# Cross-attention block: the mask of the first two pairs laid into PSUM by TensorE, and the maximum taken and subtracted by VectorE

## The chip, the cores and the metric

The kernel runs on one NeuronCore of a Trainium2 chip. The metric is the device time of one execution in microseconds (us), on that core. The core's engines work side by side, each through its own instruction stream in program order: TensorE (PE in the profile; its weight loads are PEld), VectorE (DVE), ScalarE (ACT), GpSimd (POOL) and SyncE (SP, which here only issues transfers). TensorE's results go to PSUM, which the kernel uses in banks of 512 fp32 values per partition (four singly, four as two pairs); VectorE and ScalarE read them from there.

## The reference, cut to what matters

One cross-attention block over 128 sequences of 128 tokens with 256 features and 16 heads of 16 features each, then a feed-forward network. Everything is fp32.

```python
q = (query @ Wq + bq)  # k, v from the context, in the same way; 16 heads
scores = jnp.einsum('bhqd,bhkd->bhqk', q, k) / jnp.sqrt(jnp.float32(D_K))
allowed = j < i + mask                    # mask is 0: strictly below the diagonal
scores = jnp.where(allowed, scores, NEG_INF)
attn = jax.nn.softmax(scores, axis=-1)
attn = attn.at[:, :, 0, :].set(0.0)
ctx = jnp.einsum('bhqk,bhkd->bhqd', attn, v)
x = layer_norm(query + ctx @ Wo + bo, ln1_g, ln1_b)
out = layer_norm(x + relu(x @ W1 + b1) @ W2 + b2, ln2_g, ln2_b)
```

## The kernel before

The 128 sequences are worked on in 64 **pairs** p of two sequences. The kernel's Python code writes out, engine by engine, one fixed order of instructions: each call in the main part appends to the streams of the engines that it uses, and an instruction that waits holds up what stands behind it in its stream. So the order of the calls is the schedule. Pairs 0 and 1 and the beginning of pair 2 have an order of their own, written out call by call (lines 681 to 784); after that `step(p)` repeats for p = 2 to 62, each step working on three pairs at different stages, and a last part (from line 911) drains.

The attention of one pair is split into two halves of the queries. The **high half** (`hi` = 1) holds queries 64 to 127 of both sequences on the 128 partitions, against all n = 128 keys; the **low half** (`hi` = 0) holds queries 0 to 63 against n = 64 keys, since the later keys are masked for them. For each half:

- `scores` (line 316) takes two tiles `pss` of two PSUM banks each (`sps[0]`, `sps[1]`) and fills them with 32 small matmuls; each of the four strips r of 32 rows writes into its own bank. The tiles come from a pool of two (`ps_2`), so a half can't begin before both tiles of the half before it have been read by all their readers. The other four banks (`ps_1`) serve everything else, in turns.
- `mask` (line 340), once per tile t, is a VectorE instruction that adds the mask tile `neg` (0 or -1e30) to the scores and writes `sm` in SBUF. After it the tile of PSUM is free.
- `maximum` (line 352) reduces `sm` to the negated maximum `nmx` on VectorE (line 356), and Pool adds it to `sm` (line 357). `ONE` and `TWO` are the two groups of eight heads of the high half, `ALL` all sixteen heads of the low half.
- `exponential` (line 362) runs on ScalarE, `sums` (line 368) on VectorE (a sum and a reciprocal) and Pool (the product, line 378).
- For pairs 0 and 1 `turn_on_pe` (line 410) turns the probabilities with TensorE transposes `ptp` and ScalarE copies `pT`; later pairs go through VectorE and transfers. `weigh` (line 428) multiplies them with the values into `pc`, `context` copies them, `attention_out` (`po`) applies Wo, and `attention_sum`, `attention_stats` and `norm1` make the first layer norm, whose result `x1` is turned (`turn_x1_on_pe`, `ptn`) for `hidden` (`ph`) and `second` (`py`), the feed-forward network.

Projections are `queries` (`pq`, then `qT` on ScalarE), `keys` (`pk`, `kT`) and `values` (`pv`, then `values_out` on ScalarE: two copies `vz`, a transfer issued on ScalarE's queue, a copy `vd`).

At the very start, TensorE runs 12 transposes of the identity into a bank `warm` that nobody reads (line 682), then the transposes `ptx` and `ptc` of pair 0's tokens, its projections and `scores(0, 1)`. The tile `neg` is made by Pool (lines 166 to 172).

Of the kernel before, what the change touches and what calls it, by code (L numbers as in the profile page):

```python
# [10 lines left out]
ALU = mybir.AluOpType  # L11
AX = mybir.AxisListType

P = 128
# [5 lines left out]
def tile_cross_attention_block(  # L20
# [22 lines left out]
    nc = tc.nc  # L43
# [5 lines left out]
    KC = D // P  # L49
    FC = DFF // P  # L50
    TP = 2 * P
    NS = P // 32
    HH = H // 2
    NP = B // 2
    HP = P // 2
# [19 lines left out]
    states = {}  # L75
# [62 lines left out]
    ident = const.tile([P, P], F32, tag="ident", name="ident")  # L138
# [27 lines left out]
    neg = const.tile([P, 2, HP], F32, tag="neg", name="neg")  # L166
# [46 lines left out]
    def bank(name):  # L213
        return ps_1.tile([P, 512], F32, tag="ps1", name=name)

    def pair(name):
        return ps_2.tile([P, 2, 512], F32, tag="ps2", name=name)
# [24 lines left out]
    def tokens(p, which):  # L242
        st = states.setdefault(p, {})
        st[which + "T"] = proj.tile([P, KC, TP], F32, tag=which + "T", name=f"{which}T_{p}")
        nc.vector.transpose(
            st[which + "T"], blocks_of.pop((which, p)).rearrange("p k u f -> p k (u f)")
        )
# [18 lines left out]
    def queries(p):  # L266
        st = states[p]
        st["qT"] = proj.tile([P, KC, TP], F32, tag="qT", name=f"qT_{p}")
        pq = project(wq, st["xT"], f"pq_{p}")
        for m in range(KC):  # L270
            nc.scalar.activation(  # L271
                st["qT"][:, m, :], pq[:, m * TP : (m + 1) * TP], AF.Identity,
                bias=bqs_c[:, m : m + 1], scale=QSCALE,
            )

    def keys(p):
        st = states[p]
        st["kT"] = proj.tile([P, KC, 2, TP], F32, tag="kT", name=f"kT_{p}")
        pk = project(wk, st["cT"], f"pk_{p}")
        for m in range(KC):  # L280
            for e in range(2):
                nc.scalar.activation(  # L282
                    st["kT"][:, m, e, :], pk[:, m * TP : (m + 1) * TP], AF.Identity,
                    bias=bkh[:, m, e : e + 1], scale=half[:, e : e + 1],
                )
# [27 lines left out]

    def scores(p, hi):

        st = states[p]
        n = P if hi else HP
        sps = [pair(f"pss{hi}_{p}_{t}") for t in range(2)]  # L320
        for m in range(KC):
            for s in range(2):
                first = s * P
                for r in range(NS):
                    strip = slice(32 * r, 32 * r + 32)
                    nc.tensor.matmul(  # L326
                        sps[r // 2][
                            s * HP : (s + 1) * HP, r % 2, m * 2 * n : (m + 1) * 2 * n
                        ].rearrange("p (e j) -> p e j", e=2),
                        st["qT"][strip, m, first + hi * HP : first + hi * HP + HP],  # L330
                        st["kT"][strip, m, :, first : first + n],
                        start=True, stop=True,
                    )
        st["sps", hi] = sps
        st["sm", hi] = soft.tile(
            [P, H, n], F32, tag=f"sm{hi}", name=f"sm{hi}_{p}", bufs=2
        )
        st["nmx", hi] = small.tile([P, H], F32, tag=f"nmx{hi}", name=f"nmx{hi}_{p}")

    def mask(p, hi, t):  # L340
        st = states[p]
        part = slice(t * HH, (t + 1) * HH)
        n = P if hi else HP
        no = neg.rearrange("p u j -> p (u j)") if hi else neg[:, 1, :]
        nc.vector.tensor_tensor(  # L345
            st["sm", hi][:, part, :].rearrange("p (r n) j -> p r n j", r=2),
            st["sps", hi][t][:, :, : 4 * n].rearrange("p r (n j) -> p r n j", j=n),
            no[:, None, None, :].to_broadcast([P, 2, 4, n]),
            ALU.add,
        )  # L350

    def maximum(p, hi, part):
        st = states[p]
        n = P if hi else HP
        sm, nmx = st["sm", hi], st["nmx", hi]
        nc.vector.tensor_reduce(nmx[:, part], sm[:, part, :], AX.X, ALU.max, negate=True)  # L356
        nc.gpsimd.tensor_tensor(  # L357
            sm[:, part, :], sm[:, part, :],
            nmx[:, part, None].to_broadcast([P, part.stop - part.start, n]), ALU.add,
        )  # L360

    def exponential(p, hi, part):
        sm = states[p]["sm", hi]
        nc.scalar.activation(sm[:, part, :], sm[:, part, :], AF.Exp)  # L364

    ALL, ONE, TWO = slice(0, H), slice(0, HH), slice(HH, H)

    def sums(p, hi, part):

        st = states[p]  # L370
        sm = st["sm", hi]
        n = sm.shape[2]
        su = small.tile([P, H], F32, tag=f"su{hi}", name=f"su{hi}_{p}_{part.start}")
        rs = small.tile([P, H], F32, tag=f"rs{hi}", name=f"rs{hi}_{p}_{part.start}")
        su, rs = su[:, part], rs[:, part]
        nc.vector.tensor_reduce(su, sm[:, part, :], AX.X, ALU.add)  # L376
        nc.vector.reciprocal(rs, su)  # L377
        nc.gpsimd.tensor_tensor(  # L378
            sm[:, part, :], sm[:, part, :],
            rs[:, :, None].to_broadcast([P, part.stop - part.start, n]), ALU.mult,  # L380
        )
# [28 lines left out]
    def turn_on_pe(p, hi, ts):  # L410

        st = states[p]
        sm = st["sm", hi].rearrange("p h j -> p (h j)")
        if "pT" not in st:
            pT = soft.tile([P, NS, (H + HH) * 32], F32, tag="pT", name=f"pT_{p}")
            st["pT"] = pT.rearrange("p i (n a) -> p i n a", a=32)
        for t in ts:
            pt = bank(f"ptp{hi}_{p}_{t}")
            for i in range(4):
                at = (4 * t + i) * P  # L420
                nc.tensor.transpose(pt[:, i * P : (i + 1) * P], sm[:, at : at + P], ident)
            n = 4 * t if hi else H + 4 * t
            nc.scalar.copy(  # L423
                st["pT"][:, :, n : n + 4, :].rearrange("p i n a -> p n i a"),
                pt.rearrange("p (n i a) -> p n i a", i=NS, a=32),
            )
# [63 lines left out]
    def attention_sum(p):  # L490
        st = states[p]
        t1 = st["t1"] = ffn.tile([P, 2, D], F32, tag="t1", name=f"t1_{p}")
        nc.vector.tensor_tensor(
            t1, st.pop("po").rearrange("p (s d) -> p s d", s=2), st.pop("xb"), ALU.add
        )

    def attention_stats(p):
        stats(p, states[p]["t1"], 1)
        deviation(p, 1)
# [105 lines left out]
    def add_values(ps):  # L605
        nc.vector.scalar_tensor_tensor(bov_r, ps[:, :D], live, bo_r, ALU.mult, ALU.add)
# [72 lines left out]


    warm = bank("warm")
    for i in range(12):
        nc.tensor.transpose(warm[:, i % 4 * P : (i % 4 + 1) * P], ident, ident)
    states[0] = {}
    for which, first in (("x", tokens_of[0][:, 0:2]), ("c", c_first[:, 0:2])):
        st = states[0]
        st[which + "T"] = proj.tile([P, KC, TP], F32, tag=which + "T", name=f"{which}T_0")
        pt = transposed(first, f"pt{which}_0")
        nc.vector.tensor_copy(st[which + "T"].rearrange("p k i -> p (k i)"), pt)
# [14 lines left out]
    for m in range(KC):  # L704
        pk = bank(f"pk_0_{m}")
        for k in range(KC):
            nc.tensor.matmul(
                pk[:, :TP], wk[:, k, m * P : (m + 1) * P], st["cT"][:, k, :],
                start=(k == 0), stop=(k == KC - 1),
# [16 lines left out]
    for which, first in (("x", tokens_of[0][:, 2:4]), ("c", c_first[:, 2:4])):  # L726
        st = states[1]
# [2 lines left out]
        nc.scalar.copy(st[which + "T"].rearrange("p k i -> p (k i)"), pt)  # L730
    values(0)
    values_out(0)
    mask(0, 1, 0)
    maximum(0, 1, ONE)
    mask(0, 1, 1)
    maximum(0, 1, TWO)
    exponential(0, 1, ONE)
    queries(1)
    scores(0, 0)
    mask(0, 0, 0)  # L740
    mask(0, 0, 1)
    maximum(0, 0, ALL)
    exponential(0, 1, TWO)
    sums(0, 1, ONE)
    keys(1)
    sums(0, 1, TWO)
    exponential(0, 0, ALL)
    values(1)
    ps_bv = fold_values()
    sums(0, 0, ALL)  # L750
    scores(1, 1)
    mask(1, 1, 0)
    add_values(ps_bv)
    maximum(1, 1, ONE)
    turn_on_pe(0, 1, range(2))
    values_out(1)
    turn_on_pe(0, 1, range(2, 4))
    mask(1, 1, 1)
    maximum(1, 1, TWO)
    add_bo(0)  # L760
    turn_on_pe(0, 0, range(2))
    tokens(2, "x")
    scores(1, 0)
    exponential(1, 1, ONE)
    weigh(0)
    context(0)
    mask(1, 0, 0)
    mask(1, 0, 1)
    maximum(1, 0, ALL)
    tokens(2, "c")  # L770
    attention_out(0)
    exponential(1, 1, TWO)
    sums(1, 1, ONE)
    attention_sum(0)
    attention_stats(0)
    exponential(1, 0, ALL)
    queries(2)
    sums(1, 1, TWO)
    keys(2)
    norm1(0)  # L780
# [130 lines left out]
    p = NP - 1  # L911
# [34 lines left out]
    p = NP - 1  # L946
# [34 lines left out]
    st = states[NP - 1]  # L981
    t2 = ffn.tile([P, 2, D], F32, tag="t2", name="t2_last")
    for s in range(2):
        py = bank(f"py_last_{s}")
        for f in range(FC):
            nc.tensor.matmul(
                py[:, :D], st["hT"][:, f, s * P : (s + 1) * P], w2[:, f, :],
                start=(f == 0), stop=(f == FC - 1),
# [46 lines left out]
```

## Time and profile before

| what | us |
|---|---|
| median of 3 runs | 1587.69 |
| lowest and highest run | 1587.53, 1588.26 |
| the profiled execution | 1589.6 |
| its span, from first to last instruction | 1587.9 |
| granted TensorE clock, mean | 1.00 |

The profile describes the one profiled execution. Its span is 1.7 us shorter than that execution's own time, and its time is 1.9 us above the median of the runs that were taken without a profile, so differences of a few us between kernels are read from places within the span, not from the totals. A line of the timeline has a start, a duration, the engine, the source line, the operation, the tile written and the tile read with their shapes, a count (xN: N instructions merged) and, in brackets, how long the engine had been idle before and who released it. Matmuls overlap in the pipeline: a row's duration is longer than the distance from its start to the next start, and the starts are what to measure by.

### The profile page before, as it was taken

What the parts mean: (1) busy time and instruction counts of PE and PEld (TensorE: products, weight loads), DVE (VectorE), ACT (ScalarE), POOL (GpSimd) and SP (SyncE); (2) the same over time, 40 slices, a digit from 0 to 9 for tenths busy, and PEclk for the clock granted to TensorE, in tenths of its full rate; (3) what the DMA queues carried; (4) which work ended last, traced back from release to release, by engine and by line L of the source; (5) the groups of instructions that cost most, each with busy time, mean ns of one, the idle gap of its engine ahead of it and who ended that gap; (6) DMA issues with size and microseconds to landing.
All of it is one profiled execution on the core that took longest, in us unless ns stands there. A gap on an engine that the chain in (4) does not pass through costs nothing.

```text
span 1587.9 us, 41272 instructions
## 1 busy us (share of the span) xinstructions
PE 1574.0 (99%) x16512; PEld 1327.2 (84%) x16512; DVE 1372.9 (86%) x1990; ACT 757.1 (48%) x1498; POOL 1281.9 (81%) x1104
## 2 busy tenths in 40 slices
PE   8999999999999999999999999999999999999998
PEld 6788888888888888888888888888888888888887
DVE  7999888888888988898898988888889989889872
ACT  5555445444444454454444544544444455445442
POOL 7878888788887888888888888888888888888883
PEclk9999999999999999999999999999999999999999
DMA  9555665655556556556556565565555655654521
GB/s 198 108 137 126 151 143 120 147 124 136 147 126 144 137 125 157 138 121 148 129 135 150 127 146 127 118 157 130 138 133 124 154 147 121 144 137 108 127 78 34
DMA packets 479935, 210.12 MB, mean 132 GB/s; under 512 B 348672, under 2 KB 448256, under 8 KB 479744
## 3 DMA queue, kind: packets, MB, share of 16 engines
q1 hardware_dynamic: 371104, 134.29, 38.3%
q10 hardware_dynamic: 108640, 73.19, 17.9%
q8 instruction: 131, 2.15, 0.6%
q14 instruction: 60, 0.49, 0.1%
HBM read 70.00 MB, written 33.03 MB: 65 GB/s over the span
## 4 chain that ended last, share of the span: by engine, by line
PE 92%; DVE 2%; DMA 2%; POOL 1%; SPq 1%; issue 1%; ACT 0%; ACTq 0%; POOLq 0%; DVEq 0%
PE ph L646 27%; PE py L664 26%; PE pq L260 7%; PE po L467 7%; PE pv L292 7%; PE pk L260 6%; PE pss L326 6%; PE pc L448 3%; PE pc L438 2%; DMA pT<-tb 1%; SPq L406 1%; DMA x1t<-tbx 0%; DVE sm L345 0%; DVE su L376 0%; DMA vd<-vz 0%
## 5 line engine op out<-in xcount | busy, mean ns | idle before, releaser
L357 POOL TENSOR_TENSOR sm<-sm,nmx 128x1024 f32<-128x1024 f32 x192 | 364.3, 1897 | 117.1 <-DVE nmx L356 115.3
L646 PE MATMUL ph<-x1T,w 128*128 128x256 f32 x2048 | 453.3, 379 | 0.1
L664 PE MATMUL py<-w,hT 128*128 128x256 f32 x2016 | 452.9, 382 | 0.5 <-ACT hT L652 0.4
L378 POOL TENSOR_TENSOR sm<-sm,rs 128x1024 f32<-128x1024 f32 x192 | 364.4, 1899 | 93.9 <-DVE rs L377 92.3
L664 PEld LDWEIGHTS py<-w,hT 128*128 128x128 f32 x2016 | 377.6, 190 | 73.7 <-issue 16.2
L646 PEld LDWEIGHTS ph<-x1T,w 128*128 128x128 f32 x2048 | 388.8, 190 | 53.6 <-ACT pT L423 0.5
L652 ACT ACTIVATE hT<-ph,b1e_c 128x256 f32<-128x256 f32 x504 | 209.0, 472 | 203.8 <-PE ph L646 107.9
L364 ACT ACTIVATE sm<-sm 128x1024 f32<-128x1024 f32 x192 | 200.7, 1054 | 207.9 <-POOL sm L357 199.9
L376 DVE TENSOR_REDUCE su<-sm 128x8 f32<-128x1024 f32 (+1 forms) x192 | 233.7, 1217 | 70.0 <-ACT sm L364 67.7
L345 DVE TENSOR_TENSOR sm<-pss,neg 128x1024 f32<-128x1024 f32 (+1 forms) x256 | 235.2, 939 | 48.7 <-PE pss L326 48.4
L391 DVE STREAM_TRANSPOSE tb<-sm 128x1024 f32<-128x1024 f32 x183 | 220.1, 1227 | 27.9 <-POOL sm L378 27.8
L356 DVE TENSOR_REDUCE nmx<-sm 128x8 f32<-128x1024 f32 (+1 forms) x192 | 234.3, 1220 | 6.6
L542 ACT ACTIVATE t<-t,nb,sd 128x256 f32<-128x256 f32 x124 | 67.7, 593 | 187.8 <-DMA pT<-tb 132.1
L260 PE MATMUL pq<-xT,wq 128*128 128x256 f32 x512 | 127.8, 392 | 0.0
L282 ACT ACTIVATE kT<-pk,bkh,half 128x256 f32<-128x256 f32 x252 | 120.8, 558 | 3.6 <-PE pk L260 3.6
L467 PE MATMUL po<-wo,cxT 128*128 128x256 f32 x512 | 121.1, 379 | 0.7 <-ACT cxT L460 0.7
L292 PE MATMUL pv<-wv,cT 128*128 128x256 f32 x512 | 121.0, 379 | 0.0
L260 PE MATMUL pk<-cT,wk 128*128 128x256 f32 x504 | 119.2, 379 | 0.0
L326 PE MATMUL pss<-kT,qT 32*64 32x256 f32 (+1 forms) x4096 | 116.6, 334 | 1.1 <-issue 0.7
L271 ACT ACTIVATE qT<-pq,bqs_c 128x256 f32<-128x256 f32 x128 | 53.7, 470 | 121.2 <-PE pq L260 116.5
L260 PEld LDWEIGHTS pq<-xT,wq 128*128 128x128 f32 x512 | 92.5, 190 | 20.8 <-issue 10.3
L521 POOL TENSOR_TENSOR x1b<-x,g_r 128x512 f32<-128x512 f32 x64 | 81.7, 1277 | 34.9 <-DVE x L513 34.9
(93 smaller groups left out, 1765.7 us busy)
## 6 DMA issues: line engine op xcount, KB each, us to landing
pT<-tb SPq DMA_DIRECT2D x488, 96.0 KB, 2.9
pT<-tb ACTq DMA_DIRECT2D x488, 96.0 KB, 2.7
out_dram<-t ACTq DMA_DIRECT2D x63, 256.0 KB, 2.5
xb<-in_x_dram SPq DMA_DIRECT2D x124, 128.0 KB, 4.4
cb<-in_ctx_dram SPq DMA_DIRECT2D x124, 128.0 KB, 4.3
x<-in_x_dram SPq DMA_DIRECT2D x31, 512.0 KB, 5.1
x1t<-tbx SPq DMA_DIRECT2D x248, 64.0 KB, 2.3
x1T<-x1t SPq DMA_DIRECT2D x62, 256.0 KB, 3.2
```

What stands on the lines that cost most here:

```text
L260: nc.tensor.matmul(ps[:, m * TP : (m + 1) * TP], w[:, k, m * P : (m + 1) * P], src[:, k, :], start=(k == 0), stop=(k == KC - 1),)
L292: nc.tensor.matmul(pv[:, s * D : (s + 1) * D], st["cT"][:, k, s * P : (s + 1) * P], wv[:, k, :], start=(k == 0), stop=(k == KC - 1),)
L326: nc.tensor.matmul(sps[r // 2][s * HP : (s + 1) * HP, r % 2, m * 2 * n : (m + 1) * 2 * n].rearrange("p (e j) -> p e j", e=2), st["qT"][str ...
L345: nc.vector.tensor_tensor(st["sm", hi][:, part, :].rearrange("p (r n) j -> p r n j", r=2), st["sps", hi][t][:, :, : 4 * n].rearrange("p r ...
L356: nc.vector.tensor_reduce(nmx[:, part], sm[:, part, :], AX.X, ALU.max, negate=True)
L357: nc.gpsimd.tensor_tensor(sm[:, part, :], sm[:, part, :], nmx[:, part, None].to_broadcast([P, part.stop - part.start, n]), ALU.add,)
L376: nc.vector.tensor_reduce(su, sm[:, part, :], AX.X, ALU.add)
L378: nc.gpsimd.tensor_tensor(sm[:, part, :], sm[:, part, :], rs[:, :, None].to_broadcast([P, part.stop - part.start, n]), ALU.mult,)
L391: nc.vector.transpose(st["tb"][:, :, at : at + 256].rearrange("p j (n a) -> p n j a", a=32), st["sm", hi].rearrange("p h j -> p (h j)")[:, ...
L467: nc.tensor.matmul(po[:, s * D : (s + 1) * D], cxT[:, k, s, :], wo[:, k, :], start=(k == 0), stop=(k == KC - 1),)
L646: nc.tensor.matmul(ph[:, i * TP : (i + 1) * TP].rearrange("p (s i a) -> p s i a", s=2, a=32), w1[:, k, (f + i) * P : (f + i + 1) * P], st[ ...
L664: nc.tensor.matmul(st["py"][:, s * D : (s + 1) * D], st["hT"][:, f, s * P : (s + 1) * P], w2[:, f, :], start=(f == 0), stop=(f == FC - 1),)
```

## The change

For pairs 0 and 1 (`p < 2`) the mask is no longer added by VectorE. A new function `lay` takes the two PSUM tiles and, for each of the four banks, runs one full matmul with the identity as weights and the mask, repeated four times, as the moving operand: 512 columns for the high half, 256 for the low half. The score matmuls of those pairs then accumulate onto it (`start=False`). A new function `peak` replaces `mask` and `maximum`: VectorE reduces the tile of PSUM to `nmx`, and VectorE adds `nmx` to the same tile of PSUM, writing `sm`. Pool's pass of line 357 is gone for these two pairs; Pool keeps the product in `sums`.

`lay(0, 1)` stands ahead of pair 0's token transposes, and eight of the twelve `warm` transposes are dropped. The other three calls of `lay` are made inside `scores`. The order of the calls for pairs 0 and 1 is rewritten: the exponentials come sooner, `sums` and `keys(1)`, `add_values`, `scores(1, 0)` and `queries(2)` change places with their neighbours. From `step(2)` on nothing changes.

```diff
-    def scores(p, hi):
+    def lay(p, hi):
         n = P if hi else HP
         sps = [pair(f"pss{hi}_{p}_{t}") for t in range(2)]
+        if p < 2:
+            no = neg.rearrange("p u j -> p (u j)") if hi else neg[:, 1, :]
+            for r in range(NS):
+                nc.tensor.matmul(
+                    sps[r // 2][:, r % 2, : 4 * n].rearrange("p (n j) -> p n j", j=n),
+                    ident, no[:, None, :].to_broadcast([P, 4, n]), start=True, stop=False,
+                )
+        return sps
+
+    def scores(p, hi):
+        st = states[p]
+        n = P if hi else HP
+        sps = st.pop(("laid", hi), None) or lay(p, hi)
...
-                        start=True, stop=True,
+                        start=p >= 2, stop=p >= 2 or m == KC - 1,
...
+    def peak(p, hi, t):
...
+        nc.vector.tensor_reduce(nmx, sp, AX.X, ALU.max, negate=True)
+        nc.vector.tensor_tensor(
+            st["sm", hi][:, part, :].rearrange("p (r n) j -> p r n j", r=2),
+            sp, nmx[:, :, :, None].to_broadcast([P, 2, 4, n]), ALU.add,
+        )
...
-    for i in range(12):
+    for i in range(4):
...
+    states[0]["laid", 1] = lay(0, 1)
...
-    mask(0, 1, 0)
-    maximum(0, 1, ONE)
-    mask(0, 1, 1)
-    maximum(0, 1, TWO)
+    peak(0, 1, 0)
     exponential(0, 1, ONE)
+    peak(0, 1, 1)
     queries(1)
     scores(0, 0)
-    mask(0, 0, 0)
-    mask(0, 0, 1)
-    maximum(0, 0, ALL)
     exponential(0, 1, TWO)
     sums(0, 1, ONE)
+    peak(0, 0, 0)
+    peak(0, 0, 1)
+    sums(0, 1, TWO)
     keys(1)
-    sums(0, 1, TWO)
     exponential(0, 0, ALL)
     values(1)
     ps_bv = fold_values()
     sums(0, 0, ALL)
     scores(1, 1)
-    mask(1, 1, 0)
-    add_values(ps_bv)
-    maximum(1, 1, ONE)
     turn_on_pe(0, 1, range(2))
     values_out(1)
     turn_on_pe(0, 1, range(2, 4))
-    mask(1, 1, 1)
-    maximum(1, 1, TWO)
+    add_values(ps_bv)
+    peak(1, 1, 0)
     add_bo(0)
     turn_on_pe(0, 0, range(2))
+    exponential(1, 1, ONE)
+    peak(1, 1, 1)
     tokens(2, "x")
     scores(1, 0)
-    exponential(1, 1, ONE)
     weigh(0)
     context(0)
-    mask(1, 0, 0)
-    mask(1, 0, 1)
-    maximum(1, 0, ALL)
+    exponential(1, 1, TWO)
+    sums(1, 1, ONE)
+    peak(1, 0, 0)
+    peak(1, 0, 1)
+    exponential(1, 0, ALL)
     tokens(2, "c")
     attention_out(0)
-    exponential(1, 1, TWO)
-    sums(1, 1, ONE)
     attention_sum(0)
+    queries(2)
     attention_stats(0)
-    exponential(1, 0, ALL)
-    queries(2)
     sums(1, 1, TWO)
     keys(2)
     norm1(0)
```

More of the change, by code (lines that the diff above doesn't have):

```diff
@@ L310, in values_out @@
         )
+    def lay(p, hi):
+        n = P if hi else HP
+        sps = [pair(f"pss{hi}_{p}_{t}") for t in range(2)]
+        if p < 2:
[6 more added lines that the diff above has]
+        return sps
     def scores(p, hi):
@@ L319, in scores @@
         n = P if hi else HP
-        sps = [pair(f"pss{hi}_{p}_{t}") for t in range(2)]
+        sps = st.pop(("laid", hi), None) or lay(p, hi)
         for m in range(KC):
@@ L349, in mask @@
             ALU.add,
+        )
+    def peak(p, hi, t):
+        st = states[p]
+        part = slice(t * HH, (t + 1) * HH)
+        n = P if hi else HP
+        sp = st["sps", hi][t][:, :, : 4 * n].rearrange("p r (n j) -> p r n j", j=n)
+        nmx = st["nmx", hi][:, part].rearrange("p (r n) -> p r n", r=2)
+        nc.vector.tensor_reduce(nmx, sp, AX.X, ALU.max, negate=True)
+        nc.vector.tensor_tensor(
+            st["sm", hi][:, part, :].rearrange("p (r n) j -> p r n j", r=2),
+            sp, nmx[:, :, :, None].to_broadcast([P, 2, 4, n]), ALU.add,
         )
```

## The prediction

> **What bounds the kernel now.** I read the page first (engine totals, then the chain that ended last), then TensorE's waits in the first 75 us, busy time by stretch, and the timeline of the stretch that the change touches.
>
> ```profile
> PE 1574.0 (99%) x16512; PEld 1327.2 (84%) x16512; DVE 1372.9 (86%) x1990; ACT 757.1 (48%) x1498; POOL 1281.9 (81%) x1104
> ...
> PE 92%; DVE 2%; DMA 2%; POOL 1%; SPq 1%; issue 1%; ACT 0%; ACTq 0%; POOLq 0%; DVEq 0%
> ```
>
> TensorE is busy for 1574.0 of 1587.9 us and is 92% of the chain. In the steps from 72 us on the chain is TensorE alone, so whatever moves the moment at which TensorE enters them (the value product of pair 2, at 70.96) moves the end by as much. Only the first 71 us matter, and there only TensorE's added work and its waits. The waits of TensorE in 0 to 75 us (total, times, longest):
>
> ```profile
> PE ptp L421 <- POOL sm L378: 2.5, 3, 0.9
> PE warm L683 <- POOL ident masks.py:199: 1.4, 1, 1.4
> PE pc L438 <- DMA x1t<-tbx: 0.8, 1, 0.8
> PE pc L438 <- ACT pT L423: 0.7, 2, 0.5
> PE po L467 <- ACT cxT L460: 0.7, 1, 0.7
> ```
>
> The 2.5 us for Pool's product are what pairs 0 and 1 can win. By stretch (length, then busy time of PE, PEld, DVE, ACT, POOL; granted clock):
>
> ```profile
> 16.50:21.63 5.13, 5.13 (x53) 4.16 (x52) 4.82 (x7) 4.65 (x9) 3.76 (x3) 1.00 0.98 262
> 21.63:31.44 9.81, 6.66 (x185) 5.11 (x184) 9.26 (x13) 6.96 (x14) 9.54 (x7) 1.00 1.15 250
> 31.44:38.55 7.11, 7.11 (x33) 6.00 (x33) 6.87 (x13) 4.43 (x8) 6.63 (x6) 1.00 0.72 102
> ```
>
> TensorE has 3.15 us free between 21.63 and 31.44 and none on either side. VectorE has 0.55 us free there. So the two engines that get the new work are the full ones, and Pool, which loses it, is not the only thing that fills that stretch.
>
> **The change, part by part.**
>
> *Removed.* Six Pool passes of line 357 at 1.897 us (mean of six), 11.4 us in all. They are on the way from scores to probabilities; what they delay is the Pool product ahead of each `ptp`. Eight warm transposes: their starts are 0.213 us apart (1.93, 2.14, 2.35 ...), 1.7 us.
>
> *VectorE: nothing in sum.* Before, a high tile costs one mask (1.20) and one maximum (1.22); after, one maximum and one subtraction of the same 1024 values. A maximum out of PSUM and this subtraction have no row; the nearest are the maximum out of SBUF (1.22) and the mask out of PSUM (1.20 to 1.23). Between 1.1 and 1.35 each I take 1.22 and 1.23. Four passes over two tiles, starting 1.26 and 1.13 us apart in turn as masks and maxima do, take 4.9 us. What changes is when PSUM comes free: after two passes per tile, not after one.
>
> *TensorE, layings.* The nearest row is a 128x256 fp32 matmul, which starts every 0.216 us at full pace (`pk`: 8.41 to 10.1). A laying of the low half is 4 of these, 0.86; of the high half 4 of twice the columns, 1.73. The layings inside `scores` are (0,0), (1,1) and (1,0): 3.46 us. Bounds: 1.7 if they ran at half of that, 6.9 if the repeated operand ran at half pace; I take the nearest row.
>
> *The front, `lay(0, 1)`.* These are the rows:
>
> ```profile
> 0.00:4.27 4.27, 2.82 (x12) 2.42 (x13) 0.16 (x1) 1.49 (x2) 3.15 (x18) 1.00 0.53 153
> ...
> 1.45 2.82 PE L683 MATMUL warm<-ident 128*128 128x128 f32 x12 [1.45 <-POOL ident masks.py:199]
> 4.27 1.12 PE L226 MATMUL ptx<-ident,x 128*128 128x128 f32 x4
> 6.17 2.41 PE L260 MATMUL pq<-xT,wq 128*128 128x256 f32 x8
> 8.41 1.89 PE L707 MATMUL pk<-cT,wk 128*128 128x256 f32 x8
> ```
>
> Four transposes end at 2.35 and `neg` is ready at 2.13. The granted clock reads 1.00; by it the laying takes 1.73, ends at 4.08, before the tokens come at 4.27, and costs nothing. The Trainium skill ("TensorE: Matmul & The Clock Gate", Part 1: The HAM clock gate) says that the array begins at half rate until it has been busy for a window of about 3.4 us, and the starts decide for it: the transposes here are 0.213 apart against 0.13 to 0.15 later (`ptp`: 8 in 1.04), and `pq` starts at 6.17, 6.76, 7.12, then every 0.21, so full pace came at about 7.05. At half pace a 512-column matmul takes 0.853 (4 x 0.213), the laying 3.41, and ends at 5.76: **`ptx` is 1.49 late**. Then `ptx` and `ptc` and VectorE's copy `xT` follow as before, `pq` starts at 7.63, but now at full pace: 1.75 in place of 2.24. `pk` starts at 9.38, not 8.41: **+1.0**. From there the chain (`kT`, `pss`, VectorE) is late by that. Ends: +1.5 if full pace comes only later, -0.6 in rival B.
>
> *Pair 0's low half.* All times from here are without the +1.0. `pq` of pair 1 ends issuing at 16.5 as before. VectorE's two peaks run 12.16 to 17.1, so the second half of `lay(0,0)` waits some 0.2; scores (0,0) start at 17.6, not 16.5. `pk`, `pv`, `ps_bv` behind it have no waits: `lay(1,1)` starts at 22.6, the scores (1,1) at 24.35, done at 25.5 (before: 21.63, done 22.75). ScalarE's first exponential can't come much sooner than 16.77: in its stream stand `vz`, a transfer issue and `vd`, which end there. But the second comes at 18.7, the products at 19.4, 23.4 and 25.3 (before 21.74, 23.6, 25.5). All three are done when `ptp` starts at 25.4. **The three waits for Pool (2.5) are gone**, and the `ptp` end at 28.5, as before.
>
> *What is late next.* VectorE and TensorE before:
>
> ```profile
> 21.63 1.12 PE L326 MATMUL pss<-kT,qT 32*64 32x256 f32 x32
> ...
> 24.33 1.16 DVE L345 TENSOR_TENSOR sm<-pss,neg 128x1024 f32<-128x1024 f32 x1
> ...
> 26.92 1.22 DVE L345 TENSOR_TENSOR sm<-pss,neg 128x1024 f32<-128x1024 f32 x1
> ...
> 27.41 1.09 PE L421 MATMUL ptp<-ident,sm 128*128 128x128 f32 x8 [0.77 <-POOL sm L378]
> ...
> 28.43 0.69 PE L326 MATMUL pss<-kT,qT 32*64 32x128 f32 x32
> ```
>
> The tiles came free at 28.1, just ahead of 28.43. After the change the peaks (1,1) start at 25.6 and end at 30.5. The first two matmuls of `lay(1,0)` go at 28.5, and the other two wait until 30.5: **a new TensorE wait of 1.6 us**, with the scores (1,0) and `weigh(0)` queued behind. They start at 30.95 and 31.6 (before 28.43 and 29.05): +2.5. It balances: 3.46 of work, less 2.5 and some small waits, plus 1.6 and 0.2.
>
> *To the steady part.* `po` follows at 33.9 (31.44). TensorE is then full up to `ptn` at 39.6 to 40.1, where it waits 0.19 for `x1`. VectorE's stream up to `x1`: the exponential (1,1) is done at 32.1 (behind ScalarE's `pT` copies), sum, peaks (1,0), `cT`, sum of `po`, statistics, sum, norm: `x1` at 42.3 to 42.5 for 40.07. The second instruction of line 508 still waits for the Pool product beside it (0.49 and 2.12 us for equal work). TensorE gets there 2.5 late, VectorE 2.3: the 0.19 wait vanishes, **+2.3** goes on. From `hidden(0)` on VectorE waits for TensorE's scores (47.08 after 0.88 idle), so all engines of step 2 move together and the waits at 51 and 70.96 stay.
>
> **Sum.** 1.0 + 2.3 = 3.3 us. The profiled execution would have a span of 1591.2 for 1587.9; the runs, 1587.69 + 3.3 = **1591.0**. A measurement here can tell about 0.2% (3.2 us) from no change, so the forecast lies on that line.
>
> **Rivals.**
> A. *The layings fall wholly into TensorE's holes: not slower.* For: 3.46 us of work against 3.15 us of idle. It decides at the second half of `lay(1,0)`: if VectorE has left the tiles (1,1) by 28.9, there is no 1.6 wait. That needs the scores (1,1) done by 23.9; against it, TensorE has no hole ahead of them. The whole, with the front hidden, is 3.46 - 3.15 = +0.3, and 0.3 from the later waits (1.7 in all) brings it to 1587.7; all of them, to 1586.3. Half of it, with the front at +0.3, gives some 1589.
> B. *Full pace comes with the layings.* The same page (Part 4: PE-mode transpose) says that transposes do not count as busy in the same way. For: full pace came 0.9 us after the first matmuls that weren't transposes. Then a gate that looks every 3.4 us would open at 3.64, one look earlier; the laying ends at 4.7, everything after runs at full pace, `pk` starts at 7.8: -0.6. Sum +1.7: 1589.4. Against: the look that ended at 7.05 held mostly transposes.
> C. *The new passes cost more.* If VectorE's passes out of PSUM take 1.35, the four behind `lay(1,0)` add 0.5 and the two more's worth of (1,0) 0.3 on the way to `x1`: +0.8. If the repeated moving operand runs slower by half, the layings add 1.7. For: neither has a row. Against: the nearest rows. Between the two, +1.4: 1592.4.
>
> **Chances.** Forecast 0.57 (own range 1590.2 to 1592.0, some 0.62 of it over the line, since what I may have missed, a wait or a weight load, adds), B 0.15, C 0.16, A 0.12. Range 1588.6 to 1592.8: A's better part and C's end are outside. Faster by over 0.2% would need more than the best of A: 0.04. Slower: 0.35 of the forecast, all of C, 0.01 of B: 0.52. Within: the rest, 0.44.
>
> **What would show it.** `ptx` starting near 5.8 and `pk` near 9.4; no wait of `ptp` for Pool before 31 us; a wait of some 1.6 us of a laying for VectorE's subtraction near 30 us; `po` 3.5 us later than 31.44; the value product of pair 2 at 74.3 in place of 70.96, and the same 24.2 us steps after it. It is wrong if `ptx` starts before 5, if `lay(1,0)` doesn't wait, or if VectorE's maximum takes much over 1.25.

## The result, and the profile after

| | before | after |
|---|---|---|
| median (4 runs each) | 1587.97 | 1596.64 |
| lowest, highest | 1587.53, 1590.45 | 1594.61, 1597.74 |
| span of the profiled execution | 1587.9 | 1594.4 |
| its time | 1589.6 | 1596.14 |

The change costs 8.7 us: the ratio is 1.0051, with a 95% interval of 1.0035 to 1.0066. The forecast was 3.3 us, with 5.1 as the upper end of the range (1592.8 against 1587.69). So the sign was right, and the forecast was less than half of what was measured. Between the two profiled executions the difference is 6.5 us. The kernel before was run some 90 times more beside the experiments, at medians of 1588.6 to 1588.7 and with single runs between 1586.4 and 1591.4. Against those the change costs 8.0.

The page of the changed kernel, engine totals and then the chain by engine:

```profile
PE 1582.1 (99%) x16536; PEld 1330.7 (83%) x16536; DVE 1374.7 (86%) x1992; ACT 756.9 (47%) x1498; POOL 1270.7 (80%) x1098
...
PE 95%; DVE 2%; DMA 1%; ACT 1%; POOL 1%; issue 0%; SPq 0%; POOLq 0%; DVEq 0%; ACTq 0%
```

Pool lost 11.2 us, as worked out, and VectorE nearly kept its time (1.8 us more). TensorE gained 8.1 us of busy time, and 24 more instructions than before. That second number is the first clue: four calls of `lay` with four matmuls each make 16, less 8 warm transposes, so 8 would be expected.

TensorE in the first 77 us of the changed kernel (timeline of that engine; start, duration, then what it is):

```profile
2.35 4.82 PE L323 MATMUL pss<-neg,ident 128*128 128x512 f32 x8
7.01 0.60 PE L226 MATMUL ptx<-ident,x 128*128 128x128 f32 x4
...
10.22 1.89 PE L734 MATMUL pk<-cT,wk 128*128 128x256 f32 x8
...
18.21 1.89 PE L323 MATMUL pss<-neg,ident 128*128 128x256 f32 x8
...
25.07 3.60 PE L323 MATMUL pss<-neg,ident 128*128 128x512 f32 x8
28.60 1.12 PE L339 MATMUL pss<-kT,qT 32*64 32x256 f32 x32
...
33.13 0.66 PE L447 MATMUL ptp<-ident,sm 128*128 128x128 f32 x4 [0.94 <-ACT vd L307]
33.62 2.23 PE L323 MATMUL pss<-neg,ident 128*128 128x256 f32 x8
...
38.70 1.99 PE L493 MATMUL po<-wo,cxT 128*128 128x256 f32 x8 [0.76 <-ACT cxT L486]
...
76.95 0.56 PE L464 MATMUL pc<-pT,vd 128*32 128x64 f32 x16
```

Each laying is four calls in the code and **eight** records here. From start to next start the high one takes 3.5 us (25.07 to 28.60) and the low one 1.8 (18.21 to 20.03), where the forecast had 1.73 and 0.86. The row of 512 columns is the right width and the right pace per record; there are twice as many.

Two rows of the kernel before, to compare with:

```profile
31.44 1.99 PE L467 MATMUL po<-wo,cxT 128*128 128x256 f32 x8 [0.68 <-ACT cxT L460]
...
70.96 0.45 PE L438 MATMUL pc<-pT,vd 128*32 128x64 f32 x16 [0.79 <-DMA x1t<-tbx]
```

The steps of the loss, from the two timelines: `pk` is 1.8 late (10.22 for 8.41), `po` 7.3 late (38.70 for 31.44), pair 2's value product 6.0 late (76.95 for 70.96), the end 6.5 late. Between `po` and the product 1.3 us came back: the waits for `x1` and for the transfers of pair 2 went, since TensorE was the later one. After it 0.5 came on top; the profile shows 1.7 us of stalls in three `pq` that nothing releases ("issue"), against one of 0.7 us before. That 0.5 tells nothing about the change: behind pair 2's product the instructions are the same in all ten kernels of this document, and in their traces that rest took between 1514.5 and 1517.5 us.

### The profile page after: what moved, and what is told of

Same layout as the page of the kernel before. It is cut to its first block, busy times and chain, and to the rows that moved or that the text cites. A ratio compares the mean times of both kernels' runs of the same rounds, so it can differ in the third digit from the quotient of the medians.

```text
span 1594.4 us, 41318 instructions
## 1 busy us (share of the span) xinstructions
PE 1582.1 (99%) x16536; PEld 1330.7 (83%) x16536; DVE 1374.7 (86%) x1992; ACT 756.9 (47%) x1498; POOL 1270.7 (80%) x1098
## 4 chain that ended last, share of the span: by engine, by line
PE 95%; DVE 2%; DMA 1%; ACT 1%; POOL 1%; issue 0%; SPq 0%; POOLq 0%; DVEq 0%; ACTq 0%
PE ph L672 27%; PE py L690 27%; PE pq L260 7%; PE po L493 7%; PE pv L292 7%; PE pk L260 7%; PE pss L339 7%; PE pc L474 3%; PE pc L464 2%; PE pss L323 1%; DVE sm L358 0%; DVE nmx L382 0%; DMA pT<-tb 0%; DVE su L402 0%; PE ptp L447 0%
## 5 line engine op out<-in xcount | busy, mean ns | idle before, releaser
L383 POOL TENSOR_TENSOR sm<-sm,nmx 128x1024 f32<-128x1024 f32 x186 | 352.9, 1898 | 114.3 <-DVE nmx L382 111.9
L358 DVE TENSOR_TENSOR sm<-pss,neg 128x1024 f32<-128x1024 f32 x248 | 227.8, 939 | 53.7 <-PE pss L339 53.5
L382 DVE TENSOR_REDUCE nmx<-sm 128x8 f32<-128x1024 f32 x186 | 227.0, 1220 | 6.4
```

The lines of the kernel that those rows point to most:

```text
L358: nc.vector.tensor_tensor(st["sm", hi][:, part, :].rearrange("p (r n) j -> p r n j", r=2), st["sps", hi][t][:, :, : 4 * n].rearrange("p r ...
L383: nc.gpsimd.tensor_tensor(sm[:, part, :], sm[:, part, :], nmx[:, part, None].to_broadcast([P, part.stop - part.start, n]), ALU.add,)
```

## The experiments

**Theory 1**: the loss is TensorE's time for the layings, since an fp32 matmul call is two records and so costs twice what the sum had. **Theory 2**: it is the new order and PSUM tiles held for two passes of VectorE.

### The layings in bf16

```diff
+    ident16 = const.tile([P, P], BF16, tag="ident16", name="ident16")
+    nc.vector.tensor_copy(ident16, ident)
+    neg16 = const.tile([P, 2, HP], BF16, tag="neg16", name="neg16")
+    nc.vector.tensor_copy(neg16, neg)
...
-                    ident, no[:, None, :].to_broadcast([P, 4, n]), start=True, stop=False,
+                    ident16, no[:, None, :].to_broadcast([P, 4, n]), start=True, stop=False,
```

> The changed kernel, with the identity and the mask in bf16 for the layings alone (the mask is 0 or about -1e30, the scores stay fp32). Theory 1: the cost is TensorE time of the layings, because each fp32 matmul call is recorded twice (4 calls of queries are 8 records), so a high laying is 3.46 us and a low one 1.73, 6.9 in sum ahead of the value product of pair 0. With one record per call and half the time per column the layings inside scores fall to about 1.7 us and the first one ends before the tokens come. Then ptx starts near 4.3, the value product of pair 2 near 71 to 72 (before 70.96, after 76.95), and the time is within 2 us of the kernel before, not 8 above it. Theory 2: the cost is the new order and the PSUM tiles being held for two passes of VectorE. Then TensorE waits for VectorE in place of the shorter layings, pair 2's product stays above 74 and the time at least 4 us above before.

Measured: 1590.10 (12 runs), 1.0009 times before [1.0000, 1.0017], so 6.5 us under the changed kernel. `ptx` starts at 4.24 and pair 2's product at 71.53. TensorE's timeline:

```profile
22.01 1.03 PE L329 MATMUL pss<-neg,ident 128*128 128x512 bf16 x4
22.97 1.12 PE L345 MATMUL pss<-kT,qT 32*64 32x256 f32 x32
...
28.00 0.38 PE L329 MATMUL pss<-neg,ident 128*128 128x256 bf16 x2
29.29 0.38 PE L329 MATMUL pss<-neg,ident 128*128 128x256 bf16 x2 [0.92 <-DVE sm L379]
```

The same four calls are four records and take 0.96 us for 3.5. Apart from two small copies at the start nothing else was altered, so 6.5 of the 8 to 8.7 us hang on what the fp32 layings take of TensorE. By the places, 2.2 of them are there by `pk` (7.97 for 10.22) and 6.2 by `po` (32.53 for 38.70). The last row shows what Theory 2 speaks of, a wait for VectorE's subtraction, and its size, 0.92.

### The fp32 layings alone, in the kernel before

The three layings inside `scores` are added ahead of the scores, which overwrite them (`start=True`); order, mask and subtraction are those of before.

```diff
+        if p < 2 and (p, hi) != (0, 1):
+            no = neg.rearrange("p u j -> p (u j)") if hi else neg[:, 1, :]
+            for r in range(NS):
+                nc.tensor.matmul(
+                    sps[r // 2][:, r % 2, : 4 * n].rearrange("p (n j) -> p n j", j=n),
+                    ident, no[:, None, :].to_broadcast([P, 4, n]), start=True, stop=True,
+                )
```

> The kernel before (its order, mask on VectorE, subtraction on Pool, 12 transposes) with the three fp32 layings ahead of the scores (0,0), (1,1) and (1,0) added; the scores overwrite them. So their TensorE time alone. Theory 1: 8 records each, 1.73 + 3.46 + 1.73 = 6.9 us, of which the three waits of TensorE for Pool's products (2.5) are taken up: po at 35.5 to 36.5 in place of 31.44, pair 2's product 3.7 to 4.5 late, time +3.5 to +4.5. If a laying cost what the prediction said (3.46 in all), po would be at 32.4 and the time +1.

Measured: 1593.19 (11 runs), +4.5 us against 1588.65, ratio 1.0028 [1.0020, 1.0037]. TensorE's timeline:

```profile
22.53 3.60 PE L324 MATMUL pss<-neg,ident 128*128 128x512 f32 x8
...
35.74 1.99 PE L474 MATMUL po<-wo,cxT 128*128 128x256 f32 x8 [0.68 <-ACT cxT L467]
```

`po` is at 35.74 as expected from eight records, and not at 32.4. The front of this execution was quick (`pk` at 7.68 for 8.41), so the distance from `pk` to `po` says more: 28.06 us for 23.03. That is 6.9 for the layings, less 2.5 for the waits for Pool, of which none is left, plus 0.33 and 0.50 for two new waits for ScalarE (5.2 by this sum, 5.0 measured). Pair 2's product is 3.0 late (73.98), where 3.7 to 4.5 was expected; the quick front hides 0.7. All this without `peak` and without the new order.

### The front alone

```diff
-    for i in range(12):
+    for i in range(4):
...
+    first_pair = [pair(f"pss1_0_{t}") for t in range(2)]
+    no = neg.rearrange("p u j -> p (u j)")
+    for r in range(NS):
+        nc.tensor.matmul(
+            first_pair[r // 2][:, r % 2, :].rearrange("p (n j) -> p n j", j=P),
+            ident, no[:, None, :].to_broadcast([P, 4, P]), start=True, stop=True,
+        )
+    states[0]["laid", 1] = first_pair
```

> The kernel before, with 4 warm transposes and then the four fp32 layings of the first tiles, which the scores overwrite. So the front of the change alone, without what it is for. Theory 1: the laying is 8 records, ends at about 7.0, ptx starts at 7.0 in place of 4.27 and pk at 10.2 in place of 8.41; that delay is carried to the steady part: product of pair 2 about 72.5 to 72.8, time +1.8 us. Rival: the front has slack (waits of TensorE for Pool and transfers later on take it up): product of pair 2 below 71.4 and time within 0.5. For the clock: if matmuls that aren't transposes open it sooner, the records speed up near 4.8 as in the changed kernel and not at 7.05.

Measured: 1590.76 (11 runs), +2.1, ratio 1.0016 [1.0007, 1.0025]. `ptx` at 6.91, `pk` at 10.12, pair 2's product at 72.49. The front costs about 2 us by itself. The records speed up at about 4.6, near the 4.8 of the changed kernel; that this is because they aren't transposes is not shown (see the rivals below).

### Neither layings nor mask

```diff
-        if p < 2:
+        if False:
...
-                        start=p >= 2, stop=p >= 2 or m == KC - 1,
+                        start=True, stop=True,
```

> The changed kernel without any laying; the scores of pairs 0 and 1 start their banks themselves, so these two pairs are computed without the mask. The new order, the peaks on VectorE and the four warm transposes stay. Theory 1 (the layings' TensorE time): nearly all of the loss goes, pair 2's value product starts between 70.5 and 72, the time is within 2 us of before. A wait of TensorE for VectorE's subtraction ahead of scores (1,0) of some 1 to 2 us should now be seen, since VectorE sets when the tiles are free. Theory 2 (order and held tiles): at least half of the loss stays, product at 74 or later, time at least 4 us above before.

Measured: 1592.95 (15 runs), ratio 1.0024 [1.0016, 1.0032], pair 2's product at 73.90. **This misses Theory 1's expectation**: +4.3, where at most 2 was expected, though TensorE has less to do than in the bf16 version, and it is near what Theory 2 gave (product at 74 or later, at least 4 us). The wait for VectorE is there (1.11 us ahead of scores (1,0)), but `pk` starts at 9.70, too, and that has nothing to do with pairs 0 and 1. So the front of this kernel had to be tried by itself.

### Four warm transposes

```diff
-    for i in range(12):
+    for i in range(4):
```

> The kernel before with 4 warm transposes in place of 12, nothing else. The tokens come at about 4.25 either way, so by work alone nothing changes. If an idle TensorE between 2.6 and 4.25 delays the moment at which it gets its full pace, the projections of pair 0 run at half pace for longer, as in the run without layings (keys from 9.9 in place of 8.4), and the time is +1 to +1.5 us. If the transposes have no part in it, keys start at 8.4 and the time is within 0.5 of before.

Measured: 1590.79 (12 runs), +2.1, ratio 1.0011 [1.0002, 1.0019]. TensorE's timeline:

```profile
4.31 1.11 PE L226 MATMUL ptx<-ident,x 128*128 128x128 f32 x4 [1.75 <-DMA x<-in_x_dram]
...
6.21 3.58 PE L260 MATMUL pq<-xT,wq 128*128 128x256 f32 x8
...
9.63 1.89 PE L707 MATMUL pk<-cT,wk 128*128 128x256 f32 x8
```

The tokens come when they came before, yet the eight `pq` now take 3.4 us from 6.21 to 9.63, 0.43 each, half pace to the end. So after standing idle from 2.6 to 4.3, TensorE got its full pace later here. The +2.1 is more than the +1 to +1.5 expected, which its interval (0.3 to 3.0 us) contains; in the profiled execution pair 2's product is 1.7 late (72.66). That explains half of the miss: without layings and with the same late front, order and passes cost 1592.95 - 1590.79 = 2.2 us.

### The order alone

The operations of before, 12 warm transposes, in the new order.

```diff
-    peak(1, 1, 0)
+    mask(1, 1, 0)
+    maximum(1, 1, ONE)
```

(so for all peaks; no laying)

> The operations of the kernel before (12 warm transposes, mask on VectorE, subtraction on Pool, no laying) in the order of the changed kernel. Theory 1: the order costs little by itself, within 1.5 us either way; product of pair 2 between 69.5 and 72.5. Theory 2: the order is a good part of the loss: product at 73 or later and time +3 us or more. With the subtraction on Pool the exponentials that the order pulls forward wait for Pool, so some loss is likely, about +0.5 to +1.5.

Measured: 1590.87 (20 runs), +2.2, ratio 1.0018 [1.0011, 1.0024]; product at 72.45. The product is where Theory 1 had it, the time is more than the 1.5 that it allowed, and there is a wait that I had not thought of:

```profile
25.88 3.65 PE L447 MATMUL ptp<-ident,sm 128*128 128x128 f32 x16 [2.94 <-DVE bov_r L632]
```

The new order moves `add_values` behind `turn_on_pe`. It is the last reader of the bank `ps_bv`, and the turns need that bank: the single banks are four. In the changed kernel VectorE reads it at 27.01, before the late scores (1,1) end, so there the wait is covered.

The wait is not the whole loss. The profile's row for 24.9 to 31.7 us (length, then busy time of PE, PEld, DVE, ACT, POOL; then the granted clock) reads a clock of 0.50:

```profile
24.90:31.70 6.80, 5.82 (x92) 5.09 (x96) 6.60 (x9) 4.23 (x8) 5.40 (x4) 0.50 1.11 275
```

About 2 us into the 2.94 without work the granted clock fell to half. The 16 turns behind the wait then take 3.58 us (25.88 to 29.46), where 8 of them took 0.97 before (40.50 to 41.47). From `pk` to `po` this execution is 2.7 us longer than the kernel before (25.76 for 23.03); 0.5 of that is longer waiting (2.94 for 2.5), and the other 2.2 or so are work at half pace. So the +2.2 can't be carried over as the price of the order in the changed kernel, whose trace has the full clock from 4.8 to 1592 us. How many of the 20 runs had such a stretch is not known.

### The new wait of the last turn

```diff
-    turn_on_pe(0, 1, range(2))
     values_out(1)
+    turn_on_pe(0, 1, range(2))
     turn_on_pe(0, 1, range(2, 4))
```

> The changed kernel with values_out(1) moved ahead of the first turns of pair 0 on ScalarE's stream. In the changed kernel the last turn ptp waited 0.94 us for the copy vd (line 307), which is the last reader of the bank of pv; the single banks are four. If that wait is a part of the loss by itself, ptp runs through, po starts 0.9 sooner than 38.70, near 37.8, and the time is 0.5 to 1.0 below that of the changed kernel (1596.6). If VectorE's two passes over the tiles of (1,1) set the next start anyway (they end at 34.67), the laying (1,0) waits for them in its place and po moves by less than 0.4.

Measured: 1596.61 (5 runs), ratio 1.0048 [1.0033, 1.0063]: no change. TensorE's timeline:

```profile
29.25 1.12 PE L339 MATMUL pss<-kT,qT 32*64 32x256 f32 x32
30.30 2.84 PE L447 MATMUL ptp<-ident,sm 128*128 128x128 f32 x24
...
35.37 1.13 PE L323 MATMUL pss<-neg,ident 128*128 128x256 f32 x4 [1.26 <-DVE sm L373]
...
39.35 1.99 PE L493 MATMUL po<-wo,cxT 128*128 128x256 f32 x8 [0.76 <-ACT cxT L486]
```

The turns run through, and the laying (1,0) waits 1.26 for VectorE in their place. The front of this execution was later (`pk` at 10.87 for 10.22), so `po` by itself tells nothing; from scores (1,1) to `po` it is 10.10 us in both kernels. VectorE's four passes over the tiles of (1,1) set that stretch, as the second branch of the expectation said.

### A version with bf16 layings for pair 0 alone

Pair 0 as in the bf16 version, pair 1 as before, in the old order from `scores(1, 1)` on.

```diff
-        if p < 2:
+        if p < 1:
...
-                        start=p >= 2, stop=p >= 2 or m == KC - 1,
+                        start=p >= 1, stop=p >= 1 or m == KC - 1,
```

> A version meant to beat both: bf16 layings and peaks for pair 0 alone, with the new order up to scores (1,1), and pair 1 as before. Layings within the scores then cost 0.43 us, no tile of pair 1 is held for two passes, and the products of pair 0 come sooner. Expected: no wait of ptp for Pool except the last (about 0.7), po at 30.9 to 31.4 (before 31.44), time within 0.8 us of before, on the side of -0.5. If it is above +1, the order of pair 0 costs something on VectorE that shows as a later mask (1,1).

Measured: 1587.70 (13 runs) beside 1588.65 (32 runs), ratio 0.9993 [0.9985, 1.0001]. `po` is at 30.31, 1.1 sooner than before and sooner than expected, but 0.9 of that is a quick front in this execution (`pk` at 7.50 for 8.41). The expectation of one wait for Pool missed: two of the three are left (0.62 and 0.77), since without a laying ahead of scores (1,1) the turns also come sooner. Its median is the lowest of all and clearly below that of the changed kernel; that it is faster than the kernel before is not shown, since the interval contains 1.

## Why the prediction was wrong, point by point

**The step that failed** is "*TensorE, layings*. The nearest row is a 128x256 fp32 matmul, which starts every 0.216 us at full pace ... A laying of the low half is 4 of these, 0.86". The row was right and the count wrong: I took a record of the profile for a call of the code. The page of the kernel before had the means to see it:

```profile
L260 PE MATMUL pq<-xT,wq 128*128 128x256 f32 x512 | 127.8, 392 | 0.0
```

`project` makes 4 calls, for 64 pairs that is 256, and the row counts 512. The layings inside `scores` cost 6.9, not 3.46. The Trainium skill ("FP8 and Floating Point Precision", TensorE Precision Notes) says that full fp32 takes four passes; the runs here agree roughly, with 3.5 us against 0.96 for the same call in bf16. The prediction did name 6.9 as an upper bound, for another reason, and then left it out of the range.

This one term is nearly all of the miss. At `po` the forecast stood at 3.5 late and the kernel at 7.3. The 3.8 between are 3.5 for the layings inside `scores` and 0.8 for the front, less 0.5, since the waits of the layings and of the turn ahead of them came to 1.3 (0.94 and some 0.3) where the forecast had 1.8 (1.6 and 0.2).

**The front**: right in kind, low in size. The laying ended at 7.0, not 5.76, again since it is eight records. It would have been worse at half pace throughout (6.8 us); the records go from 0.85 to 0.43 apart at about 4.8, so full pace came sooner than the 7.05 assumed. `ptx` was 2.7 late (forecast 1.49), of which 0.9 came back by `pk` (forecast 0.5), since not only `pq` but the transposes ahead of it ran at full pace (0.11 us apart, where the forecast took 0.13 to 0.15 for that pace). `pk` was 1.8 late (forecast 1.0); the front alone measured +2.1.

**The waits for Pool** (2.5): gone, as forecast, and shown twice, in the changed kernel and with the layings alone. It is the layings that hide them, by making TensorE late: with the shorter bf16 ones a wait of 0.72 is back, and without any there are two (0.86 and 0.77).

**The new wait of a laying for VectorE** (forecast 1.6): there in the right place, but only as large where TensorE is on time: 0.92 in bf16, 1.26 after the turns were freed, and some 0.3 in the changed kernel, where a wait for the bank of `pv` (0.94) came first. That wait was not in the forecast. One takes the place of the other: with the turn freed, scores (1,1) to `po` stayed at 10.10 us.

**VectorE's passes**: right. VectorE's timeline of the changed kernel has the four passes over the tiles of (1,1):

```profile
29.79 1.23 DVE L372 TENSOR_REDUCE nmx<-pss 128x8 f32<-128x1024 f32 x1 [2.38 <-PE pss L339]
31.05 1.23 DVE L373 TENSOR_TENSOR sm<-pss,nmx 128x1024 f32<-128x1024 f32 x1
32.19 1.22 DVE L372 TENSOR_REDUCE nmx<-pss 128x8 f32<-128x1024 f32 x1
33.44 1.22 DVE L373 TENSOR_TENSOR sm<-pss,nmx 128x1024 f32<-128x1024 f32 x1
```

A maximum out of PSUM costs what it costs out of SBUF, and the pass over (1,1) is 4.9 us as forecast. The 2.38 idle ahead shows who was late: TensorE.

**"The waits at 51 and 70.96 stay"**: half wrong. Those at 51 stayed, the 0.79 at pair 2's product went, because TensorE had become late enough.

**Rivals.** A (the layings fit into the holes) is out: the holes were filled and 4.5 us were left. B (the layings bring full pace sooner, since transposes don't count) is out too: full pace did come sooner than before, but at 4.8 where B had 3.64, and its reason does not hold in these runs. With the order alone and with the layings alone the transposes halve their distance at about 4.5, before any other matmul has started (`pq` at 5.75 and 5.85). C (dearer passes) was the nearest in size, but not for its reasons: VectorE's passes cost what was forecast, and where it gave a slower moving operand 1.7 us, the second record of each fp32 call took 3.5.

**What stays open.** The parts measured alone (front 2.1, layings 4.5, order and passes 2.2) add up to 8.8 for 8.0 to 8.7. Each is uncertain by 1.3 to 2 us to both sides, so how they overlap is not resolved. Why TensorE stalls with "issue", and why the rest behind pair 2's product varies by 3 us, stays open; TensorE's idle time in that rest lies between 0.5 us (four transposes) and 2.3 us (the changed kernel), which is more than half of it.

## What to carry to other kernels

Before a row prices a new instruction, divide its count by the number of calls in the code: a call can be more than one record, and the price of a call is what is wanted. Work moved to the engine that is nearly always busy is paid in full, less only the waits that it fills; a full engine is the last place to move work to, and if it must be, the cheapest data type that holds the values comes first. A buffer read twice in place of once is held twice as long: ask who takes it next before counting the passes.

## What the runs showed that I had not expected

- TensorE's full pace comes at a moment that varies from execution to execution. The windows of the profile print a granted clock of 1.00 there, because the trace has no clock record for the first microseconds; its first record, at full clock, begins at 7.04 us before and at 4.80 in the changed kernel, and that is where the starts halve their distance. With the same 12 transposes it begins at 7.04 (before), 4.41 (order alone) and 4.18 (layings alone), and `pk` starts at 8.41, 7.58 and 7.68. With 4 transposes and then nothing it begins at 9.47 and 10.47, with `pk` at 9.63 and 9.70; with 4 and bf16 layings at 5.86 and 4.24, with `pk` at 7.97 and 7.50. So up to 0.8 us of a front is chance in a single profile, and may be a part of the 5 us over which the runs of the kernel before lie.
- An idle stretch of 2.94 us in the middle of the kernel cost more than itself: the clock stayed at half for 6.8 us (order alone).
- A single profiled execution ranks kernels badly at its end. The one with four transposes had pair 2's product 1.7 late and still took 1588.88, less than the profiled execution of the kernel before (1589.6), while its median is 2.1 above.
- The eight warm transposes are worth some 2 us (1590.79 without them, 1588.65 with them; 0.3 to 3.0 by the interval), though nothing reads what they write.
- A mask of 0 and -1e30 laid in bf16 under fp32 scores takes 0.96 us of TensorE for a half in which the fp32 laying takes 3.5.
